# Where the projection corrections of the second half of the batches stand in a fused FFN, attention, FFN kernel

## The chip, the cores and the metric

One core of a Trainium2 chip runs the whole kernel as one program. The metric is the device time of one execution in microseconds. TensorE (PE) multiplies matrices, PEld is its weight load, VectorE (DVE), ScalarE (ACT) and GpSimd (POOL) work on elements, and SyncE (SP) issues most of the DMAs. Every engine works through its own instructions in a fixed order and waits on semaphores for the others.

## The reference

x has 8 batches of 1024 tokens of 512 features, all float32. Three steps follow one another, each added to x:

```
x = x + 0.5 * ffn(layernorm(x))     # 32 experts, each takes its 8 best tokens of a batch
x = x + attention(layernorm(x))     # 16 heads of 32, linear attention
x = x + 0.5 * ffn(layernorm(x))

ffn:       probs = softmax over tokens of (x gate + gb); the 8 best tokens per expert, weighted
           and summed to one row; two layers with gelu; the row is added back to those 8 tokens
attention: q = exp(x Wq' + bq), k = exp(x Wk' + bk), v = x Wv' + bv
           num_s = q_s . sum over t <= s of k_t v_t';  den_s = q_s . sum over t <= s of k_t
           out = (num / den) Wo' + bo
```

## The kernel before, in words

The program has three stages: the first FFN (to about 820 us), the attention (to about 1970 us), the second FFN. Both FFNs stream 256 MB of expert weights.

In the attention a batch is 8 chunks of 128 tokens, and two chunks are a unit (U = 2), so a batch has 4 units. The loop in `attention` goes over batches b and chunks c. In an even chunk the next unit's projection is begun (`ahead`, a generator that is advanced by `next`), in the odd chunk it goes on. Chunk 7 therefore projects unit 0 of the next batch, chunks 1, 3 and 5 units 1, 2 and 3.

Batches 0 to 3 are projected in `project`, with the three weight matrices. For batches 4 to 7 (NB0 = 4) the products of the centred input with the q, k and v weights were computed beside the first FFN, before its output was known, and stored to DRAM (`ahead_d`). `project_rest` loads them (tile pre), and has to scale them by the row's 1/sigma and to add what the first FFN contributed to the row. This contribution has rank 32: the chosen weights pm of the batch (32 experts by tokens) times the experts' outputs, already multiplied by the weights (oW for q and k, oWv for v). Adding it is called the correction here. The steps of `project_rest` are:

- in the even chunk: bo is added to x (L631, GpSimd), 1/sigma is turned and spread over partitions by a matmul (ps_rs, L636) and copied by ScalarE (rsb), GpSimd forms pmr = pm * rsb (L646) and scales pre (L650), and SP issues the load of the next unit's pre (L702). In unit 0, SP first copies the batch's pm to four row blocks (pm4, L628).
- after two `yield`s: 8 matmuls of 32 rows for q and k (ps_qk, L663), in four row tiles, into the PSUM pair sp0, sp1; two adds on VectorE (L672); 8 exponentials on ScalarE (L675); four running sums of k over the 256 tokens (`sum_keys`, a scan, L709, one for each of four groups of heads); two matmuls for v (ps_v, L684), both on the row tile of the batch, each with a value add on VectorE that gives va (L688); and the product of q and the sums on GpSimd (`times_keys`, tile qk, L720).

The rest of a chunk: `scores` (sp, L766, into the same pair sp0, sp1) and the causal mask, one half by VectorE (am0, L777), the other by a ScalarE copy (L782) and two GpSimd selects (am1, L784); in even chunks `denominators` (ps_den, L728, from qk; reciprocal rd, L736); `turn_keys` (ps_kt, L816, kc, L818); `project_out` of the chunk before (ps_o, L880, the add on VectorE L887, statistics L314, L315); in even chunks `spread_denominators` (ps_rr, L747, ScalarE copies L754); `attend`, the heads (ps_n, L830 with am and va, L842 with the running kv; VectorE's at, L851; the kv sums ps_kv, L862, ScalarE copy L871).

Two generators run beside it and are advanced a piece at a time: `begin` of the next batch (`scatter_two`, ps_sc, L293 and L300: the first FFN's output added to the next batch's x, as two matmuls on two row tiles at once; the adds L308; statistics; at the end Sqrt and reciprocal), and `route` of the batch before (gate logits, the choice of 8 tokens, ps_pmT, ps_m, ps_mT).

PSUM tiles with tag "mm" rotate through three buffers, sp0 and sp1 have one each. Outside the first FFN, a scheduler of the framework orders the instructions of each engine within what data and buffers allow; `keep_in_program_order` marks an instruction that it may not move ahead of what the program issues before it.

## Time and profile before

| what | value |
|---|---|
| three runs | 2621.52, 2622.33, 2624.72 us; median 2622.33 |
| profiled execution | 2632.39 us, its span 2630.6 us |
| busy, share of the span: PE, DVE, ACT, POOL | 83%, 33%, 19%, 14% |
| mean granted TensorE clock | 0.91 |
| chunk 7 of batch 3 to chunk 6 of batch 7 | about 1509 to 1950 us |
| denominators of chunk 0 of batches 4, 5, 6, 7 start at | 1524.98, 1636.39, 1743.45, 1860.48 us |
| DVE's busy time from 1500 to 1980 us | 324 us of 480 |

A line of a timeline gives start and duration in us, engine, source line, operation, tile written <- tiles read, shapes and count; in brackets the engine's idle time before it and what ended it. A line of the waits gives who waited for whom, the total in us, how often, and the longest. A tenth in the row PEclk below 9 means that TensorE was granted less than its full clock in a part of that slice.

### The profile page before, as it was taken

How to read it: one execution, taken by the hardware profiler on the slowest of the kernel's cores; microseconds unless marked ns; L12 is line 12 of the kernel's file. 1: busy time of each engine (PE TensorE's matmuls, PEld its weight loads, DVE VectorE, ACT ScalarE, POOL GpSimd, SP SyncE). 2: the span in 40 equal slices, each digit the busy share in tenths (PEclk: the TensorE clock that was granted, in tenths of full speed). 3: DMA queues.
4: the chain of work that ended last, by engine and by line, in shares of the span. 5: the costliest groups of instructions: out<-in, count | busy, mean ns of one | idle time of the engine just before them, and what ended most of it. 6: DMA issues, size and time to landing. Idle time of an engine off the chain costs nothing.

```text
span 2630.6 us, 41801 instructions
## 1 busy us (share of the span) xinstructions
PE 2192.9 (83%) x18679; PEld 1161.7 (44%) x18679; DVE 869.0 (33%) x1493; ACT 500.2 (19%) x967; POOL 376.7 (14%) x345
## 2 busy tenths in 40 slices
PE   8699999998986999999999989898886656656555
PEld 5354445444533666666666655555541111111111
DVE  7311111111101443444535476767651000100002
ACT  6310000000000322222222243343430000000000
POOL 0000000000000212111122244444324000000002
PEclk9899999999997999999999988988997787777887
DMA  7699999999996000010100323323149999999995
GB/s 275 253 427 426 428 427 427 426 427 427 428 429 255 1 17 1 21 49 19 58 2 19 91 86 129 118 99 107 66 175 377 423 427 428 428 428 428 428 428 248
DMA packets 95477, 667.98 MB, mean 254 GB/s; under 512 B 18222, under 2 KB 22574, under 8 KB 58432
## 3 DMA queue, kind: packets, MB, share of 16 engines
q1 hardware_dynamic: 73792, 621.45, 57.4%
q10 hardware_dynamic: 18432, 35.66, 3.5%
q0 software_dynamic: 3072, 8.19, 0.8%
q8 instruction: 147, 2.41, 0.4%
q14 instruction: 34, 0.28, 0.0%
HBM read 614.34 MB, written 48.23 MB: 252 GB/s over the span
## 4 chain that ended last, share of the span: by engine, by line
PE 49%; issue 22%; DMA 18%; DVE 7%; ACT 3%; POOL 1%; SPq 0%; ACTq 0%; POOLq 0%; DVEq 0%
DMA w<-in_w 13%; PE ps_o L880 8%; PE ps_k L599 4%; PE ps_q L599 4%; PE ps_v L800 4%; PE ps_sk L1116 3%; PE ps_sq L1116 2%; PE p_ps L1229 2%; PE ps_n L830 2%; PE sp L766 2%; PE h_ps L1206 2%; PE ps_sv L1133 2%; PE ps_n L842 2%; DMA pg<-pmT_d,chosen_idx 1%; DVE st L314 1%
## 5 line engine op out<-in xcount | busy, mean ns | idle before, releaser
L1206 PE MATMUL h_ps<-w,mT 128*8 128x512 f32 x2048 | 287.1, 696 | 120.3 <-DMA w<-in_w 118.3
L1229 PE MATMUL p_ps<-w,pm 128*32 128x512 f32 x1024 | 177.9, 830 | 137.3 <-DMA w<-in_w 133.9
L1215 DVE STREAM_TRANSPOSE hs<-h_ps 128x512 f32<-128x512 f32 x64 | 45.9, 717 | 719.2 <-PE h_ps L1206 719.2
L880 PE MATMUL ps_o<-wo_sb,at 128*128 128x512 f32 x512 | 240.0, 613 | 0.9 <-DVE at L851 0.8
L1206 PEld LDWEIGHTS h_ps<-w,mT 128*8 128x8 f32 x2048 | 50.9, 95 | 338.2 <-issue 206.9
L1229 PE MATMUL p_ps<-w,gl 128*32 128x512 f32 x1024 | 135.1, 658 | 41.9 <-DMA w<-in_w 40.0
L590 POOL TENSOR_TENSOR xt<-xt,bo_sb 128x512 f32<-128x512 f32 x32 | 45.8, 1446 | 798.0 <-PE ps_ocT L338 737.9
L1229 PEld LDWEIGHTS p_ps<-w,pm 128*32 128x32 f32 x1024 | 35.7, 132 | 276.6 <-issue 130.8
L880 PEld LDWEIGHTS ps_o<-wo_sb,at 128*128 128x128 f32 x512 | 96.2, 198 | 101.9 <-issue 98.1
L784 POOL TENSOR_SCALAR_AFFINE_SELECT am<-am 128x512 f32<-128x512 f32 x128 | 78.7, 639 | 414.3 <-ACT am L782 272.3
L314 DVE BATCH_NORM_STATS2 st<-xt 128x6 f32<-128x512 f32 x192 | 129.3, 685 | 4.9 <-DMA xt<-in_x 2.0
L599 PE MATMUL ps_k<-xnT,wk_sb 128*128 128x256 f32 x512 | 115.3, 383 | 10.8 <-ACT xnT L339 10.8
L1222 ACT ACTIVATE pm<-a 128x128 f32<-128x128 f32 x32 | 9.9, 309 | 588.5 <-DVE a L1217 588.5
L1116 PE MATMUL ps_sq<-xcT,wq_sb 128*128 128x256 f32 x512 | 117.9, 387 | 4.0 <-ACT xcT L241 4.0
L1116 PE MATMUL ps_sk<-xcT,wk_sb 128*128 128x256 f32 x512 | 117.1, 385 | 0.0
L1133 PE MATMUL ps_sv<-wv_sb,xcT 128*128 128x512 f32 x256 | 115.6, 599 | 0.0
L800 PE MATMUL ps_v<-wv_sb,xnT 128*128 128x512 f32 x256 | 115.1, 593 | 0.0
L599 PE MATMUL ps_q<-xnT,wq_sb 128*128 128x256 f32 x512 | 115.1, 383 | 0.0
L1116 PEld LDWEIGHTS ps_sq<-xcT,wq_sb 128*128 128x128 f32 x512 | 96.4, 192 | 34.7 <-issue 17.2
L1116 PEld LDWEIGHTS ps_sk<-xcT,wk_sb 128*128 128x128 f32 x512 | 96.9, 192 | 28.4 <-issue 16.2
L599 PEld LDWEIGHTS ps_k<-xnT,wk_sb 128*128 128x128 f32 x512 | 96.0, 190 | 28.2 <-ACT xnT L339 14.6
L766 PE MATMUL sp<-un 32*128 32x128 f32 x2048 | 101.9, 296 | 7.2 <-ACT un L675 6.9
(245 smaller groups left out, 2901.2 us busy)
## 6 DMA issues: line engine op xcount, KB each, us to landing
w<-in_w SPq DMA_DIRECT2D x256, 2048.0 KB, 29.9
xt<-in_x SPq DMA_DIRECT2D x31, 1024.0 KB, 10.1
pre<-ahead_d SPq DMA_DIRECT2D x16, 1536.0 KB, 6.9
ahead_d<-ahead_qk ACTq DMA_DIRECT2D x16, 1024.0 KB, 11.5
out<-xt SPq DMA_DIRECT2D x16, 1024.0 KB, 4.4
xs<-in_x ACTq DMA_DIRECT2D x16, 512.0 KB, 18.1
ahead_d<-ahead_v ACTq DMA_DIRECT2D x16, 512.0 KB, 10.9
pm<-pm SPq DMA_DIRECT2D x16, 128.0 KB, 2.4
```

The costliest lines, as they stand in the source:

```text
L314: nc.vector.bn_stats(st, xt[:, c, :])
L599: nc.tensor.matmul(ps[:, o, :], lhsT=w_sb[n][:, dc, oc * P : (oc + 1) * P], rhs=xnT[:, dc, :], start=(dc == 0), stop=(dc == NDC - 1),)
L766: nc.tensor.matmul(sp[r // 2][:, r % 2, og, :], lhsT=kT[hr, og, cols], rhs=qT[hr, og, cols], start=True, stop=True,)
L784: nc.gpsimd.affine_select(out=am[1][:, i, :, :], in_=am[1][:, i, :, :], pattern=[[0, NDC], [1, P]], compare_op=ALU.is_ge, fill=0.0, base=0 ...
L800: nc.tensor.matmul(ps, lhsT=s["xnT", b, c // U][:, dc, cols], rhs=w_sb["v"][:, dc, :], start=(dc == 0), stop=(dc == NDC - 1),)
L830: nc.tensor.matmul(ps[hr, og, :], lhsT=va[:, (og * HG + r) * HD : (og * HG + r + 1) * HD], rhs=am[r // 2][:, r % 2, og, :], start=(og == 0 ...
L842: nc.tensor.matmul(ps[hr, og, :], lhsT=kv[hr, og, :], rhs=qT[hr, og, cols], start=False, stop=True, skip_group_check=True,)
L880: nc.tensor.matmul(ps, lhsT=at[:, oc, :], rhs=w_sb["o"][:, oc, :], start=(oc == 0), stop=(oc == NDC - 1),)
L1116: nc.tensor.matmul(ps[:, o, :], lhsT=w_sb[w][:, dc, oc * P : (oc + 1) * P], rhs=xcT[:, dc, :], start=(dc == 0), stop=(dc == NDC - 1),)
L1133: nc.tensor.matmul(ps, lhsT=xcT[:, dc, i * P : (i + 1) * P], rhs=w_sb["v"][:, dc, :], start=(dc == 0), stop=(dc == NDC - 1),)
L1206: nc.tensor.matmul(h[32 * j : 32 * j + B, :], lhsT=mT[:, dc, e, :], rhs=w1h[dc // 2][:, dc % 2, j * 512 : (j + 1) * 512], start=(dc == 0), ...
L1229: nc.tensor.matmul(pp[32 * j : 32 * (j + 1), :], lhsT=gl4[e % 4][:, q, :, :].rearrange("p i b -> p (i b)"), rhs=w2h[q // (NU // 2)][:, q % ...
```

## The change

For batches 4 to 7 alone (`rest`):

- The q and k correction (matmuls, adds, exponentials) is issued at the end of the even chunk, behind its `attend`, and no longer in the odd chunk behind the scores.
- In the odd chunk `turn_keys`, the v correction and the next piece of `route` are issued ahead of `scores`; `begin` of the next batch is advanced behind `project_out` and no longer ahead of `scores`.
- `sum_keys` and `times_keys` come behind these, ahead of `attend`; the first of the four scans and the product are marked with `keep_in_program_order`.
- The two matmuls of the v correction stand on two neighbouring row tiles. For this a second copy of oWv, turned by 32 partitions (oWv1), is made by two DMAs in chunk 6 of batch 3.

```
     def project_rest(t, s, b, u):
...
             load_ahead(t, s, *divmod(b * (NCH // U) + u + 1, NCH // U))
-        yield
         yield
 
         qkT = open_unit(t, s, b, u)
...
-        sum_keys(t, s, b, u)
-
-        r = slice(32 * (b % 4), 32 * (b % 4) + E)
+        yield
+
+        ps = [t.mm.tile([P, D], F32, tag="mm", name=f"ps_v_{b}_{u * U + i}") for i in range(U)]
+        for i in range(U):
+            r = slice(E * ((b + i) % 4), E * ((b + i) % 4 + 1))
+            nc.tensor.matmul(
+                ps[i],
+                lhsT=pmr[r, i * P : (i + 1) * P],
+                rhs=s["oWv", i][r, :],
+                start=True,
+                stop=True,
+            )
         for i in range(U):
             c = u * U + i
-            ps = t.mm.tile([P, D], F32, tag="mm", name=f"ps_v_{b}_{c}")
-            nc.tensor.matmul(
-                ps, lhsT=pmr[r, i * P : (i + 1) * P], rhs=s["oWv"][r, :], start=True, stop=True
-            )
             va = t.a2.tile([P, D], F32, tag="va", bufs=3, name=f"va_{b}_{c}")
...
             s["va", b, c] = va
-        times_keys(t, s, b, u)
+        yield
+
+        sum_keys(t, s, b, u, True)
+        times_keys(t, s, b, u, True)
         yield
...
-    def sum_keys(t, s, b, u):
+    def sum_keys(t, s, b, u, pinned=False):
...
-            nc.vector.tensor_tensor_scan(
+            scan = nc.vector.tensor_tensor_scan(
...
+            if pinned and og == 0:
+                tc.keep_in_program_order(scan)
...
-        nc.gpsimd.tensor_mul(qk, s["q", b, u], s["k1", b, u])
+        product = nc.gpsimd.tensor_mul(qk, s["q", b, u], s["k1", b, u])
+        if pinned:
+            tc.keep_in_program_order(product)
...
     def attention(t, early, preload):
...
-                if c > 1:
+                nb, nu = divmod(b * (NCH // U) + c // U + 1, NCH // U)
+
+                rest = NB0 <= nb < B
+                if c > 1 and not (rest and c % U):
                     next(begun, None)
...
+                if rest and c % U:
+                    turn_keys(t, s, b, c)
+                    next(ahead)
+                    next(gate, None)
                 scores(t, s, b, c)
...
                         load_ahead(t, s, nb, nu)
+
+                        oWv = s["oWv", 1] = t.s1.tile([P, D], F32, name="oWv1")
+                        nc.sync.dma_start(oWv[E:], s["oWv", 0][: 3 * E])
+                        nc.sync.dma_start(oWv[:E], s["oWv", 0][3 * E :])
...
-                else:
+                elif not rest:
                     next(ahead, None)
                 if ("va", b, c) not in s:
                     values(t, s, b, c)
-                turn_keys(t, s, b, c)
+                if not (rest and c % U):
+                    turn_keys(t, s, b, c)
...
                 else:
+                    if rest and c > 1:
+                        next(begun, None)
                     next(ahead, None)
-                next(gate, None)
+                if not (rest and c % U):
+                    next(gate, None)
...
                 attend(t, s, b, c)
+                if rest and c % U == 0:
+                    next(ahead)
```

More of the change, by code (lines that the diff above doesn't have):

```diff
@@ L691, in project_rest @@
                 rs[:, c : c + 1],
-                ps,
+                ps[i],
                 ALU.mult,
@@ L716, in sum_keys, with times_keys @@
             )
-    def times_keys(t, s, b, u):
+            if pinned and og == 0:
+                tc.keep_in_program_order(scan)
+    def times_keys(t, s, b, u, pinned=False):
         qk = t.a1.tile([P, NDC, UT], F32, tag="qk", name=f"qk_{b}_{u}")
-        nc.gpsimd.tensor_mul(qk, s["q", b, u], s["k1", b, u])
+        product = nc.gpsimd.tensor_mul(qk, s["q", b, u], s["k1", b, u])
+        if pinned:
+            tc.keep_in_program_order(product)
         s["qk", b, u] = qk
@@ L930, in outputs_ahead @@
             evacuate(s["oW"][:, 2 * i : 2 * i + 2], ps)
-        s["oWv"] = t.ow.tile([P, D], F32, name="oWv")
+        s["oWv", 0] = t.ow.tile([P, D], F32, name="oWv")
         ps = t.mm.tile([P, D], F32, tag="mm", name="ps_oWv")
@@ L936, in outputs_ahead @@
             )
-        evacuate(s["oWv"], ps)
+        evacuate(s["oWv", 0], ps)
     def attention(t, early, preload):
@@ L1020, in attention @@
                     denominators(t, s, b, c // U)
-                    nb, nu = divmod(b * (NCH // U) + c // U + 1, NCH // U)
                     if (nb, nu) == (NB0, 0):
@@ L1033, in attention @@
                         load_ahead(t, s, nb, nu)
+                        oWv = s["oWv", 1] = t.s1.tile([P, D], F32, name="oWv1")
+                        nc.sync.dma_start(oWv[E:], s["oWv", 0][: 3 * E])
+                        nc.sync.dma_start(oWv[:E], s["oWv", 0][3 * E :])
                     if (nb, nu) > (0, 1):
-                        of = project if nb < NB0 else project_rest
+                        of = project_rest if rest else project
                         ahead = of(t, s, nb, nu) if nb < B else iter(())
                         next(ahead, None)
-                else:
+                elif not rest:
                     next(ahead, None)
```

## The prediction

> **What bounds the kernel now.** I read the 40 slices first, for where TensorE and where DMA is full; then the waits of TensorE between 1520 and 1960 us, the stretch that holds batches 4 to 7; then the timelines of TensorE, VectorE, ScalarE and GpSimd there, row by row. About 0.2% (5 us) is what a measurement of this kernel can tell from no change.

> ```profile
> PE   8699999998986999999999989898886656656555
> PEclk9899999999997999999999988988997787777887
> DMA  7699999999996000010100323323149999999995
> ```

> Each digit is a slice of 66 us. Slices 24 to 29 (from 1510 us) are the ones that the change touches: TensorE is nearly full, at a granted clock of 0.8 to 0.9, DMA is idle. From slice 30 on the second FFN waits for its weights, and its stream of 33 loads is issued only at 1967.97, after the attention. So what the attention gains or loses is taken to reach the end one to one.

> ```profile
> PE ps_den L728 <- POOL qk L720: 17.1, 8, 2.8
> PE ps_n L830 <- DVE va L688: 12.9, 12, 1.6
> PE sp L766 <- ACT un L675: 6.9, 11, 1.0
> PE ps_rr L747 <- DVE rd L736: 4.0, 2, 2.3
> ```

> Total, times and longest of TensorE's waits in that stretch: 45 us in all, 12.6 us in an ordinary batch. These are what a better order could take away. One projection in full (the unit that opens batch 5), on TensorE, VectorE and GpSimd:

> ```profile
> 1622.07 1.18 PE L766 MATMUL sp<-un 32*128 32x128 f32 x32
> 1623.17 3.70 PE L880 MATMUL ps_o<-wo_sb,at 128*128 128x512 f32 x8
> 1626.80 1.15 PE L663 MATMUL ps_qk<-pmr,oW 32*128 32x256 f32 x16
> 1627.78 1.88 PE L684 MATMUL ps_v<-oWv,pmr 32*128 32x512 f32 x4
> ...
> 1636.39 1.08 PE L728 MATMUL ps_den<-qk,hsum 128*32 128x256 f32 x8 [2.80 <-POOL qk L720]
> 1637.40 1.22 PE L636 MATMUL ps_rs<-ident,rs 128*128 128x128 f32 x4
> ...
> 1628.47 2.36 DVE L672 TENSOR_TENSOR un<-ps_qk,pre 128x1024 f32<-128x1024 f32 x2
> ...
> 1633.98 2.35 POOL L720 TENSOR_TENSOR qk<-un 128x1024 f32<-128x1024 f32 x1 [8.27 <-DVE un L709]
> ```

> The chain is correction, two adds, exponentials, sums, GpSimd's product, denominators, and TensorE idles 2.8 us at its end. Afterwards a row takes 1.08 to 1.22 us where the same one took 0.64 to 0.71 at 1524.98: half clock.

> **The change, part by part.** All durations are rows of this execution. I take times from the start of the moved correction, in the order in which the built program of the changed kernel issues. Three facts of that order carry the sum. Scores and corrections share the one pair of PSUM tiles sp0 and sp1, so scores of the odd chunk now wait for the adds. The three rotating "mm" buffers make the route's matmul (chunks 1, 3, 5) wait until the first value add has emptied the buffer. And only the first scan and the product are held back; the other three scans still go ahead of the mask, and the held scan stands behind the output projection's add and statistics, in chunks 1, 3 and 5 behind the odd chunk's heads (at) too.

> *The values' correction by two row tiles.* Before, 1627.78 to 1629.58, 1.80 us. The scatter already runs as two row tiles, and the pair takes 1547.83 to 1548.79, 0.96 us:

> ```profile
> 1547.83 0.69 PE L293 MATMUL ps_sc<-o_all,pm 32*128 32x512 f32 x1
> 1547.83 0.69 PE L300 MATMUL ps_sc<-odd 32*128 32x512 f32 x1
> 1548.36 0.59 PE L293 MATMUL ps_sc<-o_all,pm 32*128 32x512 f32 x1
> ```

> So it gives 0.84 us a unit (bounds 0 and 0.9). The two copies of oWv add two issues to SP's queue, 0.62 us each by the like ones of odd, ahead of pm4's four, whose data landed 2.7 us before GpSimd used it at 1515.06. Cost 0; at most 2.7 us, if they hold it up by the 5.4 us that odd took to land. SP's later loads of pre wait for a value add, and these come no later than before.

> *Chunk 7 (unit 0 of the next batch).* The correction ends at 0.97, values at 1.95. The first add starts at 1.24 (1515.83 to 1517.07, the one time it waited for TensorE), the second ends at 3.6: TensorE idles 1.65. Scores to 4.7, output projection to 8.3. ScalarE: exponentials 2.5 to 6.25, score copy to 7.25; GpSimd's selects to 8.55; heads 8.6 to 10.6, next scores to 11.7. VectorE: values 4.8, three scans 6.6, mask 7.75, output add from 8.35 and statistics 9.85, held scan 10.5; product 10.65 to 13.0; denominators at 13.05, after 1.35 idle. Behind the held product on GpSimd stand the next chunk's selects, which TensorE asks for only after denominators, output projection and spread, 6 us later: hidden. Before: 14.32. From denominators to gate sums 5.37 at full clock (1524.98 to 1530.35), before 6.7, 7.8 and 6.8. Sum 18.4, before 21.0, 22.1 and 21.1.

> *Chunk 1 (unit 1).* Before, from the end of chunk 0's heads to that of chunk 2's kv sums: 27.97, 25.9, 27.26 and 24.2 for batches 4 to 7. After: idle 1.7 until the first value add (4.15); output projection ends at 9.2. ScalarE now has the four logit copies (2.10) ahead of the score copy: 8.95, 9.95, selects 11.25, so heads wait 2.1 and end at 13.3. VectorE has the choice's three passes (1.18, 1.25, 1.24) ahead of the output add: 12.65; statistics 14.2, heads out 14.8, held scan 15.55, product 18.05, denominators 18.1 after 2.45 idle (before 15.6 to 17.1, hardly a wait). The rest, 8.5: 26.6.

> *Chunk 3 (unit 2).* Before 35.1, 31.5, 36.4 and 30.2. After: idle 1.7, output projection 9.35, scatter 10.3, heads 12.3, next scores 14.65. VectorE: output add, two scatter adds and three statistics to 13.65, heads out 14.25, scan 15.0. GpSimd: two bias adds to 15.5, product 17.85. Denominators 17.9, idle 3.25; rest 11.45: 29.35; 27.15 in batch 7, which has no scatter.

> *Chunk 5 (unit 3).* Before 24.87, 24.87, 27.53; batch 7's denominators at 15.6. After: idle 1.7, heads 12.7, scores 14.2. The next batch's reciprocal now stands ahead of the held scan, and waits for a Sqrt behind a table load (1.28): 15.3; scan 15.95, product 18.4, denominators 18.45, idle 4.25; rest 8.45: 26.9 (batch 7's denominators 15.8).

> *The first unit.* Correction (4,0) now stands ahead of chunk 7's scores and output projection, 4.8 us of work that filled the wait for GpSimd's pmr (1508.75 to 1515.83). Its input comes no sooner, so denominators at 1515.83 + 12.6 = 1528.4, before 1524.98: +3.5.

> *Sum at full clock.* Batch 4 +3.5 and -5.1, batch 5 -2.0, batch 6 -12.0, batch 7 -3.2: -18.8.

> *The clock.* Before had 17 waits of 1 us or more in this stretch; after 13 the rows ran at half clock, after 4 (1613.65, 1669.70, 1786.06, 1941.02) they did not. A spell cost 1.3 to 2.4 us by the stretch from denominators to gate sums, 1.6 by heads (3.6 for 2.0); I take 1.5. The times of before hold its spells, the sum above has none. After has nine gaps a batch: 1.65, 1.35, 1.7, 2.1, 2.45, 1.7, 3.25, 1.7, 4.25. The spell after chunk 1's first is lost in the wait that follows. Four of 1.35 to 1.7 at two in three (1.61 and 1.63 fell, 1.72 did not), three of 2.45 and more at three in four, half of one for the 2.1: 5.3 spells, 8 us a batch; 6 in chunks 1 to 5 of batch 4, 2.5 in its first unit (7 us idle ahead), 6.5 in batch 7: 31 us. Bounds: 0, and eight spells of 2.4. Net -18.8 + 31 = +12.

> [...]

> **The rivals.** *The clock holds: faster.* The place is the four short gaps and chunk 1's; at three spells a batch (4.5 us) the sum is nil, with none it is -18.8, 2603. For it: fewer rows behind VectorE's values, and the four waits that left the clock full. Against it: 13 of 17. *No change to be told:* three to four spells, 2621 to 2627. *The held scan costs more:* its longer gaps drop the clock nearly every time, spells of 1.8 us after seven of the eight, 12.6 us a batch, 49 in all: +30, 2652. For it: batch 6 of before, 117 us against batch 5's 107 with nearly the same work. *The change does nothing* can't be: 16 corrections move in the built order.

> **How the numbers follow.** Forecast 0.45, held scan costs more 0.15, no change 0.15, faster 0.25. The profiled execution took 2632.39 us (span 2630.6 and 1.8 around it), 10.1 above the median of 2622.33; on it the sum gives 2644, on the median 2634. Range 2610 (a third of the way from a clock that holds throughout to no change) to 2652. The forecast's own range is 2627 to 2643. Faster 0.25, same 0.15, slower 0.60.

> **What would show it.** Denominators waiting for GpSimd's product in chunks 1, 3 and 5, 2.4 to 4.3 us, where before it was chunks 5 and 7; value corrections overlapping in 1.0 us; odd scores waiting 1.7 us; heads of chunk 1 waiting for GpSimd's select; a 7 us hole ahead of the first correction. I am wrong if the held scan runs soon after the mask and denominators don't wait, or if the gaps come as told and the clock stays full.

## The result and the profile after

The changed kernel takes 2662.65 us (median of four runs, 2661.26 to 2664.65), the kernel before beside it 2621.95 us: the ratio is 1.0153, 95% interval 1.014 to 1.0165, or 40.7 us slower. Run again on another chip it took 2665.54 us against 2629.34, a ratio of 1.0129 (1.0108 to 1.015). The forecast was 2634 us, 12 us slower: the direction is right, the size is under a third of what came, and the time lies 10.7 us above the range. The kernel before had medians of 2622 to 2629 us in the comparisons below, so kernels are compared by their ratio to the runs of before beside them.

The 40 slices of the changed kernel (its profiled execution: 2661.26 us, span 2659.5):

```profile
PE   8799999998977999999999888888896655555555
PEclk9899999999998999999999888888897688787888
DMA  7699999999995000010100323323139999999996
```

The digits of PEclk below 9 now fill slices 23 to 29; before, they stood in 24, 25, 27 and 28. The attention ends later, and the second FFN runs as it did. From the last turn of 1/sigma in `route` (ps_rsT) to the end it is 661.1 us, before 662.0.

TensorE's waits in the attention's second half, 1508 to 2010 us (total, times, longest, in us):

```profile
PE ps_den L740 <- POOL qk L730: 45.8, 16, 4.4
PE ps_qk L663 <- POOL pmr L647: 6.4, 1, 6.4
...
PE ps_rs L387 <- DVE va L693: 5.2, 4, 1.3
PE ps_mT L562 <- DVE va L693: 5.2, 4, 1.3
PE ps_pmT L519 <- DVE va L693: 5.2, 4, 1.3
PE sp L778 <- DVE un L672: 3.8, 7, 0.6
```

The denominators now wait for GpSimd's product in all sixteen units, 45.8 us where it was 17.1. The heads' waits for value adds (12.9 us before) are gone; in their place each odd chunk opens with a gap, 1.3 us in chunks 1, 3 and 5 (route's matmul waits for the first value add) and 0.5 + 0.6 us in chunk 7 (scores wait for the adds). The unit that opens batch 5, as shown of before, in the timelines of TensorE, VectorE and GpSimd:

```profile
1634.13 1.15 PE L663 MATMUL ps_qk<-pmr,oW 32*128 32x256 f32 x16
1635.10 1.02 PE L683 MATMUL ps_v<-oWv,pmr 32*128 32x512 f32 x4
1636.64 0.49 PE L778 MATMUL sp<-un 32*128 32x128 f32 x4 [0.52 <-DVE un L672]
1637.77 1.16 PE L778 MATMUL sp<-un 32*128 32x128 f32 x28 [0.64 <-DVE un L672]
1638.86 5.40 PE L892 MATMUL ps_o<-wo_sb,at 128*128 128x512 f32 x8
...
1649.01 0.64 PE L740 MATMUL ps_den<-qk,hsum 128*32 128x256 f32 x8 [1.62 <-POOL qk L730]
...
1645.75 0.18 DVE L315 BATCH_NORM_AGGREGATE mv_g<-st 128x2 f32<-128x6 f32 x1
1645.85 0.66 DVE L717 TENSOR_TENSOR_SCAN un<-ones,un 128x256 f32<-128x256 f32 x1
...
1646.59 2.36 POOL L730 TENSOR_TENSOR qk<-un 128x1024 f32<-128x1024 f32 x1 [4.15 <-DVE un L717]
```

Two things are to be seen. The values' correction takes 1.02 us (before 1.88). But the output projection ps_o right behind the short gaps takes 5.40 us for the eight matmuls that took 3.70 before: half clock for part of it (the granted clock over it is 0.68). In the changed kernel 15 of the 16 output projections behind such an opening took 4.66 to 5.80 us.

Where the time went is told by splitting one stretch, from the denominators of chunk 6 in batch 3 to the last turn of 1/sigma in route, into idle time of TensorE and the time that its rows hold (start to next start, less the idle time). What the rows hold with nothing slowed, 379.0 us, is taken from the run e3 below, in which every row is at full clock (524.1 us, less 145.1 us of unread matmuls). The rest is put down to half clock.

| kernel | stretch | idle | unread matmuls | half clock |
|---|---|---|---|---|
| before | 475.0 | 50.3 | 0 | 33 to 39 (its rows hold 7 to 13 us more work: single row tiles) |
| after | 506.2 | 74.5 | 0 | 52.7 |
| e2, free scans | 453.0 | 35.9 | 0 | 38.1 |
| e7, openings filled | 485.3 | 55.4 | 30.8 | 20.1 |
| e6, both | 430.2 | 16.4 | 30.9 | 3.9 |

So in the profiled pair the stretch is 31.2 us longer: 24.2 of idle time, 14 to 20 of half clock, less the work that two row tiles save. The trace's own record of the granted clock, which counts idle time as well, agrees: half of the time at half clock in the stretch is 46.1 us before, 59.7 after, 35.8 in e2, 23.9 in e7 and 2.0 in e6.

### The profile page after: what moved, and what is told of

Same layout as the page of the kernel before. It is cut to its first block, busy times and chain, and to the rows that moved or that the text cites. A ratio compares the mean times of both kernels' runs of the same rounds, so it can differ in the third digit from the quotient of the medians.

```text
span 2659.5 us, 41781 instructions
## 1 busy us (share of the span) xinstructions
PE 2191.8 (82%) x18679; PEld 1158.4 (44%) x18679; DVE 865.7 (33%) x1493; ACT 500.6 (19%) x967; POOL 381.2 (14%) x345
## 4 chain that ended last, share of the span: by engine, by line
PE 47%; issue 23%; DMA 19%; DVE 5%; POOL 3%; ACT 3%; ACTq 0%; POOLq 0%; SPq 0%; DVEq 0%
DMA w<-in_w 14%; PE ps_o L892 9%; PE ps_k L599 4%; PE ps_q L599 4%; PE ps_v L812 4%; DMA xg<-out,chosen_idx 2%; PE ps_sk L1144 2%; PE p_ps L1257 2%; PE ps_sq L1144 2%; PE sp L778 2%; PE ps_sv L1161 2%; PE ps_n L842 2%; PE h_ps L1234 2%; POOL qk L730 2%; PE ps_n L854 2%
## 5 line engine op out<-in xcount | busy, mean ns | idle before, releaser
L1257 PE MATMUL p_ps<-w,pm 128*32 128x512 f32 x1024 | 170.0, 796 | 139.4 <-DMA w<-in_w 129.5
L892 PE MATMUL ps_o<-wo_sb,at 128*128 128x512 f32 x512 | 262.4, 660 | 0.1
L590 POOL TENSOR_TENSOR xt<-xt,bo_sb 128x512 f32<-128x512 f32 x32 | 45.8, 1446 | 795.1 <-PE ps_ocT L338 735.0
L892 PEld LDWEIGHTS ps_o<-wo_sb,at 128*128 128x128 f32 x512 | 104.6, 215 | 116.4 <-issue 112.4
L1144 PEld LDWEIGHTS ps_sk<-xcT,wk_sb 128*128 128x128 f32 x512 | 97.6, 193 | 28.5 <-issue 15.6
```

The costliest lines, as they stand in the source:

```text
L892: nc.tensor.matmul(ps, lhsT=at[:, oc, :], rhs=w_sb["o"][:, oc, :], start=(oc == 0), stop=(oc == NDC - 1),)
L1144: nc.tensor.matmul(ps[:, o, :], lhsT=w_sb[w][:, dc, oc * P : (oc + 1) * P], rhs=xcT[:, dc, :], start=(dc == 0), stop=(dc == NDC - 1),)
L1257: nc.tensor.matmul(pp[32 * j : 32 * (j + 1), :], lhsT=gl4[e % 4][:, q, :, :].rearrange("p i b -> p (i b)"), rhs=w2h[q // (NU // 2)][:, q % ...
```

## The experiments

Theory: the held scan and product make the denominators late, and each of the two gaps of a unit, opening and denominators, drops the clock behind it. Rivals: the opening gaps alone are the cost; the waits alone are it and the clock has another reason; holding the product is what hurts.

**Both marks taken off (e1).** TensorE's order stays the same.

```
-        sum_keys(t, s, b, u, True)
-        times_keys(t, s, b, u, True)
+        sum_keys(t, s, b, u)
+        times_keys(t, s, b, u)
```

> The changed kernel without the two marks on the first scan and the product; TensorE's order stays the same, the fourth scan goes ahead of the mask and the product ahead of the odd chunk's selects. If the held sums are the main cause, the denominators' waits (45.8 us in the stretch from 1508 to 2010 us) shrink to under 15 us, heads wait some 1 to 1.5 us in each odd chunk for the selects that now stand behind the product (2.35 us on GpSimd), and the time falls by 25 to 45 us, to 2618 to 2638. If the gaps that open the odd chunk (route's matmul and the scores waiting for the value adds and the adds) are the main cause, they are still there and the time stays above 2645.

2620.49 us against 2625.26, ratio 0.9981 (0.997 to 0.9992). The denominators' waits are gone altogether; heads wait for selects 1.8 us in all, less than expected. Without the two marks the changed order is no slower than before.

**Only the product held (e2).**

```
-        sum_keys(t, s, b, u, True)
+        sum_keys(t, s, b, u)
         times_keys(t, s, b, u, True)
```

> The changed kernel with only the product held in place; all four scans go ahead of the mask. If the held scan is what makes the denominators late, the product starts at the end of the selects (8.5 to 11.3 us after the correction begins, where the held scan ended at 10.5 to 16), the denominators' waits fall from 45.8 to under 10 us, most of the half-clock rows behind them go too, and the time falls by 40 to 60 us, to 2602 to 2622. If the held product alone makes the wait, nothing changes: 2655 to 2665.

2609.92 us, ratio 0.9942 (0.9923 to 0.9961). Chunk 5 of batch 4 on VectorE, GpSimd and TensorE in the changed kernel, where the correction begins at 1602.72:

```profile
1614.49 0.69 DVE L899 TENSOR_TENSOR xt<-ps_o,xt 128x512 f32<-128x512 f32 x1 [3.00 <-PE ps_o L892]
...
1619.91 0.20 DVE L983 RECIPROCAL rs<-sd 128x8 f32<-128x8 f32 x1 [0.80 <-ACT sd L982]
1620.03 0.86 DVE L717 TENSOR_TENSOR_SCAN un<-ones,un,un 128x256 f32<-128x256 f32 x1
...
1620.97 2.34 POOL L730 TENSOR_TENSOR qk<-un 128x1024 f32<-128x1024 f32 x1 [0.63 <-DVE un L717]
...
1623.37 1.08 PE L740 MATMUL ps_den<-qk,hsum 128*32 128x256 f32 x8 [4.34 <-POOL qk L730]
```

and with the scan free, where it begins at 1593.96:

```profile
1599.92 2.65 DVE L717 TENSOR_TENSOR_SCAN un<-ones,un,un 128x256 f32<-128x256 f32 x4
...
1604.10 2.35 POOL L730 TENSOR_TENSOR qk<-un 128x1024 f32<-128x1024 f32 x1
...
1611.81 0.64 PE L740 MATMUL ps_den<-qk,hsum 128*32 128x256 f32 x8
```

The held scan runs 17.3 us behind the correction's start, after VectorE has waited 3.0 us for ps_o and worked off the add, the statistics, the scatter and the reciprocal. Free, all four scans end 8.6 us behind it, the product runs in the selects' shadow, and the denominators neither wait nor run at half clock. Freeing this one instruction a unit is worth 53 us, by the stretch (506.2 to 453.0) and by the ratios (1.0153 and 0.9942 of 2622: 55). Holding the product costs nothing; e2, which holds it, is even quicker than e1, which does not (0.9942 and 0.9981, intervals apart).

**Sums held, but behind the scores (e8).** Both marks stay; only the place in the program differs.

```
                 scores(t, s, b, c)
+                if rest and c % U:
+                    next(ahead)
...
-                    next(ahead, None)
+                    if not rest:
+                        next(ahead, None)
```

> The changed kernel, both marks kept, but the sums and the product issued directly behind the odd chunk's scores and masks, no longer behind the output projection. If the held scan is late because the output projection's add, its statistics and the next batch's work stand ahead of it on VectorE, this is as good as the free scan: 2602 to 2618. If holding it behind the mask is the cost by itself, 2640 to 2662.

2607.22 us against 2622.53, ratio 0.9934 (0.9914 to 0.9954). So it is the place behind the output projection's add that costs, not the mark, nor the place behind the mask.

**Filling the gaps (e3, e5, e7, e6, e10).** Matmuls whose result nobody reads, into a free part of the bank of the kv sums:

```
+        if (b, u) == (NB0, 0):
+            fill(t, s, 26)
...
+        fill(t, s, 6)
...
+    def fill(t, s, n):
+        for _ in range(n):
+            mm = nc.tensor.matmul(
+                s["fill"],
+                lhsT=ident,
+                rhs=w_sb["o"][:, 0, :UT],
+                start=False,
+                stop=False,
+                skip_group_check=True,
+            )
+            tc.keep_in_program_order(mm)
...
+        if b >= NB0:
+            fill(t, s, (6, 12, 14, 18)[u])
...
+                s["fill"] = bank[:, UT:]
```

They stand ahead of the first correction, behind the values' correction and ahead of the denominators.

> The changed kernel with matmuls on TensorE that nobody reads, placed into its gaps: six of 128 by 256 (some 1.4 us) behind the values' correction, six, twelve, fourteen and eighteen (1.4 to 4.2 us) ahead of the denominators of units 0 to 3, twenty-six ahead of the first correction. The order of everything else is the same. If the gaps cost the clock, the output projections behind the opening gaps take 3.6 to 3.7 us and no longer 4.7 to 5.8, the rows behind the denominators 0.64 to 0.71 and no longer 1.1 to 1.2, and the time falls by 30 to 50 us, to 2612 to 2632. If the clock falls for another reason, or the waits alone are the cost, the rows stay as slow and the time is 2660 to 2672.

2689.78 us, ratio 1.0247 (1.023 to 1.0264): a miss by size, since TensorE's rows have two instructions for one such float32 matmul (52 for the 26 ahead of the first correction) and the filler was twice as long as meant (2.86 us in an opening). But with TensorE idle for only 8.6 us of the stretch every output projection took 3.70 us or less and every row of denominators 0.64. Halved, 13, 3 and (3, 6, 7, 9):

> The changed kernel with unread matmuls of about the length of its gaps: half of the count of the run with too many (opening gaps 1.43 us, denominators 1.43, 2.86, 3.3 and 4.3 us, first correction 6.2 us). The run with too many put some 68 us more on TensorE than the gaps were long and took 27 us more than the changed kernel, with every row at full clock. If the half clock behind the gaps is about half of what the change cost, this one takes 2605 to 2628, 35 to 55 us less than the changed kernel. If a shorter gap that is left behind the filler drops the clock as well, 2640 to 2660.

2630.52 us, ratio 1.0027 (1.0013 to 1.004), 2.5 us above the first range; half clock is all but gone (3.1 us by the same split), and 79.0 us of filler hold the place of the gaps. The same filler without the one ahead of the denominators:

> The changed kernel with its two marks, filler in the opening gaps and the first correction's hole alone, none ahead of the denominators. It tells the loss behind the opening gaps from that behind the denominators: if the opening gaps cost 2 to 3 us of half clock each and the denominators' chain moves up with the output projection, 2615 to 2632; if the denominators' waits grow by what is saved, 2650 to 2662.

2638.46 us, ratio 1.0053 (1.0034 to 1.0071), between the two expectations. The waits in its stretch:

```profile
PE ps_den L755 <- POOL qk L745: 45.8, 16, 4.4
PE ps_n L857 <- POOL am L811: 5.4, 8, 1.2
```

The denominators wait exactly as long as without filler: their chain hangs on the output projection and moves up with it. The heads' wait for the selects, 5.4 us, is new, 1.4 us in each chunk 1; the slow output projection had hidden it. One opening of the sixteen is still slow (5.40 us). The same opening filler with the scans free:

> All four scans free, the product held, and the opening gaps and the first correction's hole filled with unread matmuls (1.43 and 6.2 us); nothing ahead of the denominators. In the run without filler each opening gap of 1.2 to 1.3 us was followed by 2 to 3.4 us of half-clock loss. If that loss is caused by the gap, the time falls by another 25 to 45 us, to 2565 to 2585. If the freed time turns into waits for the product or the selects, 2590 to 2605. If the filler gives nothing, 2610 to 2613.

2584.22 us, ratio 0.9838 (0.9817 to 0.9859), the fastest of all. The opening of chunk 5, batch 4, on TensorE, with the filler as L713:

```profile
1594.44 1.13 PE L685 MATMUL ps_v<-oWv,pmr 32*128 32x512 f32 x4
1595.49 1.56 PE L713 MATMUL ps_kv<-wo_sb,ident 128*128 128x256 f32 x6
1597.07 1.08 PE L562 MATMUL ps_mT<-isum,m 128*128 128x32 f32 x8
1598.08 1.17 PE L793 MATMUL sp<-un 32*128 32x128 f32 x32
1599.18 3.70 PE L909 MATMUL ps_o<-wo_sb,at 128*128 128x512 f32 x8
```

The two by two adds up: filled openings are worth 1.0 points of the ratio with held scans (1.0153 to 1.0053) and 1.04 with free ones (0.9942 to 0.9838); free scans 2.1 either way. Filler and sums behind the scores:

> Both marks kept, sums issued directly behind the odd chunk's scores, and unread matmuls in the opening gaps (1.43 us) and the first correction's hole. If the two losses, held scan and half clock behind the opening gaps, add up as in the two by two of the earlier runs (24 to 26 us for the filler, 53 to 55 us for the scan), the time is 2575 to 2590. If the filler only moves the wait to the product, 2598 to 2610.

2586.38 us, ratio 0.9855 (0.9839 to 0.9872), the same as e6 within the intervals.

**The two row tiles (e4, e12).** Into the kernel before, and nothing else:

```
-        r = slice(32 * (b % 4), 32 * (b % 4) + E)
...
+            r = slice(E * ((b + i) % 4), E * ((b + i) % 4 + 1))
...
+                rhs=s["oWv", i][r, :],
...
+                        oWv = s["oWv", 1] = t.s1.tile([P, D], F32, name="oWv1")
```

> The kernel before with the values' correction on two row tiles and nothing else of the change. Eight of its sixteen pairs took 1.8 us in a block; at 1.0 each that is 7 us less, and up to 13 if the other eight, which run mixed with heads, gain as much: 2609 to 2616. If the time that it frees turns into waits for VectorE's value adds or GpSimd's product, 2620 to 2624.

2627.04 us, ratio 1.0003 (0.9993 to 1.0013): nothing. What TensorE gains comes back as waits of the heads for the value adds, 18.9 us where it was 12.9. In its profile the stretch is 468.5 us, 6.5 shorter than in the two profiles of before, but those are of executions above their median, and the medians show no gain. Taken out of the free-scan kernel:

```
-            r = slice(E * ((b + i) % 4), E * ((b + i) % 4 + 1))
+            r = slice(E * (b % 4), E * (b % 4 + 1))
...
-                rhs=s["oWv", i][r, :],
+                rhs=s["oWv", 0][r, :],
```

> All four scans free and the product held, with the values' correction back on one row tile (1.9 us a pair and no longer 1.0) and without the copy of oWv. If two row tiles gain what they take from TensorE's rows, this is 13 us slower than with them, 2620 to 2626. If the gap behind them is set by the value add on VectorE, the 0.9 us only fills a part of the gap, which falls from 1.3 to about 0.5 us: 2606 to 2614, and where the shorter gap no longer drops the clock, faster, 2575 to 2600.

2603.31 us, between the second and the third expectation, ratio 0.9919 (0.9901 to 0.9937), against 0.9942 with two tiles; the intervals overlap, the stretch is 446.5 us against 453.0. The opening gap is set by the value add on VectorE, so 0.9 us less on TensorE is 0.9 us more gap. But the clock did not do what the gap theory says:

```profile
1593.01 1.98 PE L683 MATMUL ps_v<-oWv,pmr 32*128 32x512 f32 x4
1594.84 0.38 PE L778 MATMUL sp<-un 32*128 32x128 f32 x2
1595.65 1.53 PE L562 MATMUL ps_mT<-isum,m 128*128 128x32 f32 x8 [0.44 <-DVE va L693]
1597.12 2.09 PE L778 MATMUL sp<-un 32*128 32x128 f32 x30
1599.13 5.57 PE L892 MATMUL ps_o<-wo_sb,at 128*128 128x512 f32 x8
```

The gap is 0.44 us, and everything behind it is as slow as behind 1.3 us.

**How long a gap (e11).** The kernel of e6 (its edit below is against that) with none, one, two and three unread matmuls by batch:

```
-        fill(t, s, 3)
+        fill(t, s, b - NB0)
```

> All four scans free and the product held, the first hole filled, and the opening gaps filled with none, 0.48, 0.95 and 1.43 us of unread matmuls in the projections of batches 4, 5, 6 and 7: gaps of about 1.3, 0.8, 0.35 and 0 us are left. If the clock falls with any gap of more than half a microsecond, the output projections behind the gaps take 4.7 to 5.8 us in batches 4 and 5 and 3.7 in 6 and 7; if it takes about 1.1 us, only batch 4's are slow; if the length does not matter, all but batch 7's are. Time 2590 to 2605.

One execution, 2596.81 us (before beside it 2624.17). No single length divides them: in batch 4 (gaps of 1.3 us) output projections behind them took 3.70, 6.02 and 4.76 us in chunks 1, 3 and 5, in batch 5 (0.88 us) 3.70, 4.62 and 3.70, in batch 6 (0.45 us) 3.70, 5.63 and 3.70, in batch 7 none was slow. Less gap and more matmuls go with fewer slow ones, as far as one execution tells; chunk 3 is the last to recover.

**Idle or little used (e13, e14).** The filler of e6 on 32 rows of the array in the openings, and the kernel of e12 with one unread matmul in its short gap (and the first hole filled as in e6). The first edit is against e6, the second against e2:

```
-                lhsT=ident,
-                rhs=w_sb["o"][:, 0, :UT],
+                lhsT=ident[:rows],
+                rhs=w_sb["o"][:rows, 0, :UT],
...
-        fill(t, s, 3)
+        fill(t, s, 3, E)
```

> The run with free scans and filled opening gaps, but the unread matmuls in the opening gaps use 32 rows of TensorE and no longer 128; their time on TensorE is the same, 1.4 us, so no gap is left. The hole ahead of the first correction keeps the filler of full height. If idle time drops the clock, the output projections take 3.7 us as with full height and the time is 2580 to 2590. If it is the little use of the array around the gap, they take 4.7 to 5.8 us as without filler and the time is 2600 to 2615.

```
-            r = slice(E * ((b + i) % 4), E * ((b + i) % 4 + 1))
+            r = slice(E * (b % 4), E * (b % 4 + 1))
...
+        fill(t, s, 1)
```

> Free scans, product held, the values' correction on one row tile, and one unread matmul of full height (0.48 us) in the 0.44 us gap behind it; the first hole filled. If closing the gap is what counts, every output projection takes 3.7 us and the time is 2572 to 2586. If the 32-row stretch is longer here (1.9 us and no longer 1.1) and that is what drops the clock, the projections stay at 5.1 to 5.6 us and the time is 2598 to 2606.

e13: 2604.85 us, in its second range, ratio 0.9901 (0.9879 to 0.9924). Its openings are not quite closed: 0.22 us are left in batches 4 and 7, 1.07 in 5 and 6, where the filler stands on another row tile than the correction and runs beside it. Of the projections behind the openings of chunks 1, 3 and 5, 9 of 12 took 4.3 to 6.0 us, in batches 4 and 7 alone 5 of 6; with filler of full height (e6) it is 1 of 16. Chunk 1 of batch 4:

```profile
1536.32 1.13 PE L685 MATMUL ps_v<-oWv,pmr 32*128 32x512 f32 x4
1537.29 1.45 PE L713 MATMUL ps_kv<-wo_sb,ident 32*128 32x256 f32 x6
1538.96 0.66 PE L387 MATMUL ps_rs<-rsT,pick 8*128 8x128 f32 x3 [0.22 <-DVE va L696]
...
1541.47 4.33 PE L909 MATMUL ps_o<-wo_sb,at 128*128 128x512 f32 x8
```

e14: 2599.59 us, ratio 0.9889 (0.9865 to 0.9914): the time is in its second range, but the projections are not all slow as that wanted. 10 of 16 projections are at 3.70 us; the four of chunk 3, where pmT's 32 by 32 matmuls follow on the correction, are all slow, with no gap:

```profile
1558.89 1.98 PE L685 MATMUL ps_v<-oWv,pmr 32*128 32x512 f32 x4
1560.80 0.70 PE L713 MATMUL ps_kv<-wo_sb,ident 128*128 128x256 f32 x2
1561.53 1.63 PE L519 MATMUL ps_pmT<-diag,pm 32*128 32x32 f32 x13
...
1565.12 6.30 PE L909 MATMUL ps_o<-wo_sb,at 128*128 128x512 f32 x8
```

So the idle time alone does not tell these cases apart: with no gap behind the corrections e14 has 6 slow projections of 16, and e6, with 1.4 us of filler on 128 rows, has 1; with 0.22 us left, behind filler on 32 rows, e13 has 5 of 6.

The traces also list the granted clock, as records with a start, a length and a share: 176 in the changed kernel's trace, 150 in that of before. Every share is 0.5 or 1.0, and the changes lie whole multiples of 3.413 us apart, to within 0.001 us. For each such step of 3.41 us in the stretch, add up the columns that the matmuls stream, each matmul by its share of the 128 rows, so that one on 32 rows counts a quarter (the eight matmuls of an output projection at full clock are 4096 columns in 3.70 us, some 3800 in a step). In the changed kernel's trace 23 steps at full clock had under 1530 of them, and after all 23 the clock was at half; 90 had more, and after 1 it was. Over the fourteen profiles of the changed order it is 134 of 135 and 3 of 1548. Two openings of the changed kernel with the same gap lie differently on the steps:

```profile
1810.30 1.85 PE L519 MATMUL ps_pmT<-diag,pm 32*128 32x32 f32 x15 [1.30 <-DVE va L693]
1813.17 5.38 PE L892 MATMUL ps_o<-wo_sb,at 128*128 128x512 f32 x8
...
1844.15 1.08 PE L562 MATMUL ps_mT<-isum,m 128*128 128x32 f32 x8 [1.30 <-DVE va L693]
1846.25 3.70 PE L892 MATMUL ps_o<-wo_sb,at 128*128 128x512 f32 x8
```

The first falls into one step, 1809.76 to 1813.18, with 1084 columns; the second, the only one of the sixteen that kept the clock, is cut by a border at 1843.90 into steps of 1582 and 2265. The figure of 1530 is read off the same profiles, and no run was made to test it. With the old order it divides the steps less well: in the profiles of before and e4, all 25 steps under 1530 were followed by half clock, and 21 of 304 above it too (9 of 9 and 6 of 103 in the first profile of before).

**The two kernels again (e9, e15).**

> The kernel before, unchanged, profiled a second time. In its first profile the stretch from chunk 6's denominators in batch 3 to the last turn of 1/sigma in route took 475.0 us, and the whole 2632.4 us, 10 us above its median. If that stretch varies between executions, it is 462 to 470 us in a profile near the median of 2622. If it is 475 us again, the 10 us lie in the two FFNs around it.

> The changed kernel again, on another chip. If its first four runs (2661 to 2665) were typical, the ratio to the kernel before is 1.014 to 1.0165 again. If it varies like the other kernels, by 10 us from run to run, the ratio is nearer to the 31 us of the profiled stretch: 1.010 to 1.014, 2650 to 2660.

Before: 2630.02 us with the stretch at 475.3. Both profiled executions lie 6 to 10 us above the medians beside them and have the same stretch, so it does not tell what the quicker executions do otherwise. After: ratio 1.0129 (1.0108 to 1.015), stretch 509.4 us; the ratio lies in the second range, the time of 2665.54 us above it, 36 us slower than before beside it. 14 of its 16 output projections behind openings are slow.

## Why the prediction was wrong

- *The attention's loss reaches the end one to one*: right, 662.0 and 661.1 us follow it.
- *Two row tiles give 0.84 us a unit*: right as rows (1.02 to 1.13 us for a pair), wrong as a gain: alone they give nothing (e4), and in the new order they only lengthen the gap (e12). The sums of the chunks had that in them, since their opening gap was worked out from VectorE; the 0.84 us ought not to have stood as a gain.
- *The gaps*: right. Denominators were to wait 1.35, 2.45, 3.25 and 4.25 us in the four chunks, and waited 1.62, 2.67 to 4.36, 3.3 and 4.34 (batch 7's chunks 3 and 5 1.3); the openings were to be 1.65 to 1.7 and were 1.16 to 1.3; the first hole was to be 7 and was 6.4. That the held scan stands behind the output projection's add, and in chunk 5 behind the reciprocal, is what the timelines show and e2 and e8 show it to be the cause. The heads' wait in chunk 1 stayed hidden behind the slow output projection; it shows as soon as that is at full clock (5.4 us in e7, 1.4 a time where 2.1 was forecast).
- *The sum at full clock, -18.8 us*: right within 3 us. Work and idle time of the changed kernel are 379.0 + 74.5 = 453.5 us, 21.5 less than the stretch before.
- *The clock, +31 us*: this is the step that failed, 5.3 spells a batch at 1.5 us. The mechanism was right, the term too small: the loss was 52.7 us. The denominators' share was about right: one of 1.35 us at two in three and three longer ones at three in four are 4.4 us a batch, 17.5 in all, and 20.1 us are left in e7, where the denominators' waits and one slow opening remain. By length it was wrong both ways: in the changed kernel none of the seven waits of 1.29 to 2.67 us dropped the clock and all nine of 3.24 and more did, at some 2.2 us each. The openings are the miss. Three a batch at two in three, chunk 1's at nothing (its spell was to be lost in the heads' wait), are 12 us, some 14 with the first hole; filling them and the hole took 32.6 us away (52.7 to 20.1), 1.9 us for each of the 17. They fell 15 times in 16, chunk 1's too. The share of two in three was counted over all waits of before, wherever they stood; an opening stands among the corrections' 32-row matmuls, and by e13 (9 of 12 slow), e14 (6 of 16) and the sums over the steps the slow projections go with these as well. The rival "the held scan costs more", with seven of eight gaps at 1.8 us, 49 us in all and +30, had the sum nearly right, by luck: it put the loss down to the held scan's longer waits, and most of it stood behind the openings.
- *The length of a gap*: ahead of the denominators it sorted the waits of the changed order (in the changed kernel's two profiles and e7 the clock fell behind 27 of 29 of 3.08 us and more and behind none of 19 of 2.67 and less); in the kernel before it fell behind one of three of 2.36 to 2.37 us and two of three of 2.80. The openings are not sorted by it: the clock fell behind gaps of 1.2 to 1.3 us, and in e14 with none.
- *The base*: the sum was set on the median of 2622, its durations came from an execution of 2632. With 52.7 in place of 31 the sum is +34 us, and the stretch shows 31.2. The medians differ by 36 to 41. The 5 to 10 us between are not settled: before's profiled executions are slower than its others, the changed kernel's are not.
- *Two readings of before*: of the 13 waits counted as drops, two (1576.58 and 1687.05) came with the clock already at half. The last copy of pm landed at 1513.00, 2.1 us ahead of its use and not 2.7; nothing hung on it.

So the cost is shown to be the place of one held scan (53 us) and the half clock behind the openings (24 to 27 us). With both mended the new order is 1.6% faster than the kernel before.

## What to carry to other kernels

Holding an instruction in program order holds it behind everything that is issued ahead of it on that engine, and there the last arrival counts (the held scan ran 17.3 us behind the correction's start, the four free ones ended at 8.6): put it where its inputs are ready, or leave it to the scheduler. Price a gap on TensorE with the half clock behind it, and count that as likely where narrow matmuls surround it (29 of 32 openings in the changed kernel's two profiles); a faster row ahead of a fixed wait only makes the gap longer (1.3 us behind the pair of 1.13, 0.44 behind that of 1.98). Where a short gap can't be closed, unread matmuls of full height and of its length can pay for themselves (0.9942 to 0.9838 from e2 to e6).
